# Layer 2's convolution units: x buffers in unit order, loads ahead of norms, raw strips for the last batch

## Chip, core and metric

The kernel runs on one core of one Trainium2 chip, in float32. The metric is the device time of one execution in microseconds (us). A core has five engines with queues of their own: TensorE (PE, with its weight loads as PEld), VectorE (DVE), ScalarE (ACT), GpSimd (POOL) and SyncE (SP). SP issues most DMAs here, ACT and POOL some. DMAs move data between device memory (HBM) and on-chip memory; PE writes its products to PSUM, from where ACT and DVE fetch them.

## What is computed

The input x has 4 batches, 384 channels and 64 x 64 positions. Four layers follow one another, each as x = x + f(gn(x)), where gn is a group norm without weights (32 groups, per batch). The change lies in layer 2 and at its borders:

```python
p = x.mean(axis=(2, 3), keepdims=True)            # here x is gn(x)
gate = sigmoid(sigmoid(bn(pw(gelu(bn(pw(p, dc_w1))), dc_w2))) - 0.5)
kw = softmax(bn(pw(gelu(bn(pw(p, kp_w1))), kp_w2)), axis=1)
y3 = bn(dw(x, c3_w, 1))                           # depthwise 3 x 3
y5 = bn(dw(x, c5_w, 2))                           # depthwise 5 x 5
y1 = x * c1_w + c1_b
tok = bn(kw[:, 0:1] * y3 + kw[:, 1:2] * y5 + y1)
tok = tok * sigmoid(bn(pw(gelu(bn(pw(tok.mean(...), cg_w1))), cg_w2)))
ch = tok + bn(pw(gelu(bn(pw(tok, cm_w1))), cm_w2))
return gate * ch + (1.0 - gate) * x
```

Every bn takes its mean and variance over all batches and positions, so a channel's two convolutions must be complete before its tokens can be formed, and all tokens before the matrix products that follow.

## The kernel before

The kernel is written with tile pools. A pool hands out buffers by tag (`bufs` of them), the waits between engines are generated, and the order in which instructions stand in each engine's queue is settled when the kernel is built; it need not be the order of the Python text. Channels lie on the 128 partitions, in three channel tiles j = 0, 1, 2.

**Phase A** (`phase_a`, layers 0 and 1) does attention and then layer 1, one batch at a time. The last batch's layer 1 (`layer1` with `alone`) runs by itself, in eight blocks of 512 positions. A block ends in `band_out` (L1142): for each channel tile o, two matrix products (L1148, L1149), an add on DVE into x[:, o] (L1152), then the statistics (L630) and a store of the block to x1 (L1155). When the eight blocks are done, `norm_of_stats` gives scale r2 and shift n2 of layer 2's group norm (L1026 to L1030). Beside it `strips_of` already prepares batches 0 to 2 of channel tile 0 for layer 2.

**Strips.** `open_strips` (L1161) holds z, 128 channels by 33 strips by 4 batches, with positions on the partitions and the batch innermost. A strip is a transposed 128 x 128 piece of normalised x. For channel tile 0, `strips5` (L1316) loads x1, normalises it on ACT (L1320), transposes it on PE (L1325) and copies it to z, in turn on ACT and DVE (L1331, L1329).

**Phase B** (`phase_b`, L1169) is the convolution stage. It works in 12 units of 32 channels; a unit's x tiles have 32 channels of each of four batches on the partitions. Unit u belongs to channel tile j = u // 4. Each unit has 16 steps of two channels:

- `matrices53` (L1339) forms, three steps ahead, the band matrices of a pair of channels from taps, on DVE or (odd steps) on POOL (L1351). `taps53` (L1333) loads the taps of four steps, one group ahead, by POOL (L1337), into one of three buffers.
- `conv53` (L1359) does 12 products with strips as stationary operand (L1370), two ACT copies out of PSUM (L1379, L1381), DVE statistics (L1384), and every fourth step a 1024 KB write to d53 from ACT's queue (L1386).
- `conv_norms` (L1391), after the next unit's first convolution, turns the statistics into coefficients.
- `unit_tok` (L1427) forms the tokens of the unit before, in four parts of two halves: it reads 1024 KB of convolution results back (c_d, three buffers, SP, L1436), adds on ACT and DVE into the unit's x tile (L1444, L1449, L1451), squares it (L1456) and stores the tokens (L1463).
- `unit_strips` (L1261) brings in x of a unit ahead: tile 0, then tile 1, each by eight SP loads of 128 KB (L1272), each norm on ACT for 1024 positions (L1280), then, for j > 0, transposes and copies to z (L1294, L1299, L1301).

The x tiles come from pool b_x, six buffers with one tag. A unit's two tiles are held from load to token store. `phase_b` asks for them in this order: four times for the last batch's strips of channel tile 0 (L1190), then unit 1's tile 0, unit 0's tile 0, unit 1's tile 1, unit 0's tile 1, then units 2, 3 and so on. The load of unit u + 2's first tile and its first norm come together at step 15 of unit u (L1218), its second tile at step 1 of the next unit. The token halves of unit u - 1 are drawn at the even steps of unit u and at step 15.

**The tail.** After unit 11 come its `conv_norms`, its tokens, `tok_stats` (L1466) and, in `phase_ef`, a chain of small operations up to the first product of the next stage (h_s, L1604). `phase_ef` first loads the weights w2 (cm_w2_t, 1152 KB, used only in its second half, L1660) and then w1, all from ACT's queue (L334).

## Time and profile before

| | |
|---|---|
| Runs (3), median | 4841.11 us (4838.23 to 4847.09) |
| Profiled execution | 4841.52 us |
| Its span | 4839.6 us, granted PE clock 0.95 |
| PE, DVE, ACT, POOL busy over the span | 91%, 60%, 41%, 16% |
| Last block's x1 done; norm ready | 2434.2; 2439.9 us |
| First convolution product (L1370) | 2460.19 us |
| Last unit's statistics on PE (L1402) | 3013.47 us |
| First product of the next stage (L1604) | 3067.74 us |
| Moved between 2460 and 3012 us | 154.70 MB, 280 GB/s |

Times are counted from the start of the span. A row of the timeline reads: start, length, engine and line, operation, what is written and read, count, and in brackets how long the engine was idle before and what released it. SPq is the queue from which SP issues DMAs; an issue's length is not the transfer's. In rows of stretches, the number behind each length in brackets counts instructions, and the DMA share is the mean busy share of 16 DMA engines. In a chain of waits each row is a start, a length and what that time went to.

### The profile page before, as it was taken

What the parts mean: (1) busy time and instruction counts of PE and PEld (TensorE: products, weight loads), DVE (VectorE), ACT (ScalarE), POOL (GpSimd) and SP (SyncE); (2) the same over time, 40 slices, a digit from 0 to 9 for tenths busy, and PEclk for the clock granted to TensorE, in tenths of its full rate; (3) what the DMA queues carried; (4) which work ended last, traced back from release to release, by engine and by line L of the source; (5) the groups of instructions that cost most, each with busy time, mean ns of one, the idle gap of its engine ahead of it and who ended that gap; (6) DMA issues with size and microseconds to landing.
All of it is one profiled execution on the core that took longest, in us unless ns stands there. A gap on an engine that the chain in (4) does not pass through costs nothing.

```text
span 4839.6 us, 49747 instructions
## 1 busy us (share of the span) xinstructions
PE 4399.5 (91%) x18445; PEld 2453.7 (51%) x18445; DVE 2892.0 (60%) x4647; ACT 1996.9 (41%) x2976; POOL 757.7 (16%) x643
## 2 busy tenths in 40 slices
PE   6999999999999999989987898699999997778888
PEld 2233444344443444435477787344444443678888
DVE  7766556645656455556867777555521113767898
ACT  4444444444444444336345566211133334763321
POOL 1000000000000000000044554000000001235544
PEclk9999999999999999989988999899999998788999
DMA  4312212111211111113168898776664444995776
GB/s 145 102 42 66 72 53 75 64 56 42 70 61 63 40 59 59 53 63 120 65 197 282 278 308 299 273 259 251 238 236 153 156 156 152 325 346 183 231 256 232
DMA packets 289663, 747.65 MB, mean 154 GB/s; under 512 B 22555, under 2 KB 123014, under 8 KB 277382
## 3 DMA queue, kind: packets, MB, share of 16 engines
q1 hardware_dynamic: 226744, 454.62, 29.4%
q0 software_dynamic: 36480, 167.01, 9.2%
q10 hardware_dynamic: 26190, 122.76, 6.4%
q8 instruction: 149, 2.44, 0.2%
q14 instruction: 100, 0.82, 0.1%
HBM read 442.04 MB, written 302.25 MB: 154 GB/s over the span
## 4 chain that ended last, share of the span: by engine, by line
PE 32%; DVE 7%; DMA 6%; ACT 3%; issue 2%; POOL 1%; SPq 0%; ACTq 0%; DVEq 0%; POOLq 0%
PE h_m L1658 10%; PE h_s L1604 10%; PE conv_m L1370 6%; PE conv_m L1972 2%; DMA c_d<-d 2%; DMA wmix<-in_mix_t 1%; DMA g_h<-h 1%; DVE toep L1959 1%; PE box_m L2050 1%; DVE in_x L2052 1%; DMA ax<-x 1%; DVE in_x L2062 1%; DMA unit_x<-x 1%; DVE box L2034 0%; ACT g_h L1908 0%
## 5 line engine op out<-in xcount | busy, mean ns | idle before, releaser
L819 ACT ACTIVATE probs<-sc_s 128x1024 f32<-128x1024 f32 x512 | 496.5, 1019 | 695.0 <-PE av L929 594.8
L929 PE MATMUL av<-probs,vt 128*128 128x512 f32 x1536 | 717.7, 604 | 0.0
L1128 DVE SCALAR_TENSOR_TENSOR acc<-band,vecs,acc 128x512 f32<-128x512 f32 x708 | 496.0, 745 | 44.9 <-POOL band L1089 39.6
L1658 PE MATMUL h_m<-f_h,cm_w_t 128*128 128x512 f32 x1152 | 497.3, 595 | 7.4 <-ACT f_h L1646 7.4
L1370 PE MATMUL conv_m<-toep,z 128*128 128x192 f32 (+1 forms) x2304 | 444.2, 354 | 9.5 <-DVE z L1299 9.4
L929 PEld LDWEIGHTS av<-probs,vt 128*128 128x128 f32 x1536 | 277.6, 192 | 339.6 <-issue 335.9
L1972 PE MATMUL conv_m<-toep,z 128*128 128x128 f32 x3072 | 395.5, 287 | 36.5 <-POOL toep L1959 15.8
L1370 PEld LDWEIGHTS conv_m<-toep,z 128*128 128x128 f32 x2304 | 408.5, 197 | 31.6 <-DVE z L1299 10.1
L1972 PEld LDWEIGHTS conv_m<-toep,z 128*128 128x128 f32 x3072 | 381.1, 203 | 38.4 <-POOL toep L1959 16.2
L1604 PE MATMUL h_s<-e_tok,cm_w_t 128*128 128x512 f32 x768 | 362.9, 595 | 4.2 <-DVE e_tok L1589 4.2
L1658 PEld LDWEIGHTS h_m<-f_h,cm_w_t 128*128 128x128 f32 x1152 | 220.4, 191 | 284.4 <-issue 273.3
L1666 DVE BATCH_NORM_STATS2 h_st<-f_h 128x6 f32<-128x512 f32 x96 | 66.5, 694 | 429.8 <-ACT f_h L1665 429.8
L811 PE MATMUL sc_s<-q,k 32*128 32x512 f32 x2048 | 307.1, 643 | 15.1 <-ACT probs L819 14.9
L1351 POOL TENSOR_TENSOR toep<-w,band 128x1280 f32<-128x1280 f32 x94 | 272.6, 2900 | 237.5 <-PE conv_m L1370 234.3
L1051 PE MATMUL t_m<-w_in_t,xb 128*128 128x384 f32 x768 | 282.0, 503 | 3.4 <-DVE coef L1068 3.2
L965 PE MATMUL proj_m<-xm,w_proj_t 128*128 128x512 f32 x576 | 270.3, 609 | 6.4 <-DVE xm L904 4.9
L1611 ACT COPY e_h<-h_s 128x1024 f32<-128x1024 f32 x96 | 97.2, 1012 | 400.2 <-PE h_s L1604 400.2
L1613 DVE BATCH_NORM_STATS2 h_st<-e_h 128x6 f32<-128x512 f32 x192 | 123.4, 685 | 204.9 <-ACT e_h L1611 204.7
L1604 PEld LDWEIGHTS h_s<-e_tok,cm_w_t 128*128 128x128 f32 x768 | 146.9, 191 | 187.9 <-issue 183.1
L1051 PEld LDWEIGHTS t_m<-w_in_t,xb 128*128 128x128 f32 x768 | 144.4, 194 | 141.6 <-issue 62.5
L972 DVE SCALAR_TENSOR_TENSOR x_res<-proj_m,bn_c,x_res 128x512 f32<-128x512 f32 x96 | 71.7, 747 | 240.2 <-PE proj_m L965 240.2
L1604 PE MATMUL h_s<-z,cm_w_t 128*128 128x512 f32 x384 | 196.7, 594 | 0.0
(423 smaller groups left out, 6396.3 us busy)
## 6 DMA issues: line engine op xcount, KB each, us to landing
d<-d_o ACTq DMA_DIRECT2D x48, 1024.0 KB
c_d<-d SPq DMA_DIRECT2D x48, 1024.0 KB
hid<-e_h ACTq DMA_DIRECT2D x16, 3072.0 KB
f_h<-hid SPq DMA_DIRECT2D x16, 3072.0 KB
x_in<-in_x SPq DMA_DIRECT2D x96, 256.0 KB
x_res<-in_x SPq DMA_DIRECT2D x32, 768.0 KB
xa<-x_res POOLq DMA_DIRECT2D x32, 768.0 KB, 3.9
xa_out<-xa SPq DMA_DIRECT2D x32, 768.0 KB
```

The source lines that it names most:

```text
L811: nc.tensor.matmul(s[:, g], lhsT=k4[32 * g : 32 * g + 32, c], rhs=q[i][32 * g : 32 * g + 32], start=True, stop=True,)
L819: nc.scalar.activation(p[:, h * 1024 : (h + 1) * 1024], s[:, 2 * h : 2 * h + 2].rearrange("p a b -> p (a b)"), AF.Exp, scale=0.25,)
L929: nc.tensor.matmul(av[0], lhsT=vt[:, 4 * c + v, :], rhs=p[:, v * 512 : (v + 1) * 512], start=c == 0 and v == 0, stop=c == 7 and v == 3,)
L965: nc.tensor.matmul(m, lhsT=self.w_proj[:, j, o * P : (o + 1) * P], rhs=xm[:, j], start=j == 0, stop=j == NJ - 1,)
L1051: nc.tensor.matmul(m[:, 0:C], lhsT=xb[:, j], rhs=self.w_in[:, j, :], start=j == 0, stop=j == NJ - 1,)
L1128: nc.vector.scalar_tensor_tensor(out, src(j, k), w, done, ALU.mult, ALU.add)
L1351: eng.tensor_tensor(t, self.w53[:, at : at + 160].rearrange("p (m n) -> p m n", n=8).unsqueeze(2).to_broadcast([P, 20, 8, 8]), band.rearra ...
L1370: nc.tensor.matmul(m[:, c * 256 + to : c * 256 + to + 64 * (k1 - k0)], lhsT=self.z_[:, at : at + P], rhs=t[:, 10 * c + k0 : 10 * c + k1].r ...
L1604: nc.tensor.matmul(s[:, v, :], lhsT=w1[:, j, o * P : (o + 1) * P], rhs=t[j][:, v * 512 : (v + 1) * 512], start=j == 0, stop=j == NJ - 1,)
L1613: nc.vector.bn_stats(st[:, o, 8 * b + 2 * i + v, :], h[:, o, v * 512 : (v + 1) * 512])
L1658: nc.tensor.matmul(m, lhsT=w2[:, o, j * P : (j + 1) * P], rhs=h[:, o, v * 512 : (v + 1) * 512], start=o == 0, stop=o == 5,)
L1972: nc.tensor.matmul(m[:, ch * P : (ch + 1) * P], lhsT=self.z_[:, at : at + P], rhs=t[:, 8 * c + 2 * i : 8 * c + 2 * i + 2].rearrange("p m a ...
```

## The change

- **Raw strips.** In the last batch's `band_out`, after the add of channel tile 0, `raw_strips` transposes the not yet normalised block (four transposes into a PSUM tile "m") and copies it to z by ACT.
- **Factors and scaling.** `strip_factors` builds, in phase B, the scale and shift of each of the 128 channels copied to every partition: two DVE operations, one product of 256 columns, one copy. It uses one x buffer. `scale_strips` multiplies and adds 32 channels of z in place on DVE, one quarter ahead of unit 0 and three at its steps 3, 7 and 11. The four loads, norms and strips of the last batch go.
- **Taps.** Their pool moves to `open_strips`, with two buffers for three, and the first load is issued there.
- **Order of x.** Unit 0's two tiles are asked for first (tile 0, norm, tile 1, ahead of the loop), unit 1's at steps 1 and 3. `load(0)` and `norm(0)` are apart by a yield: the load of unit u + 2 is drawn at step 11 and its norm at step 15.
- **Last unit.** Unit 10's token halves are drawn at every step from step 1 of unit 11, twice at even ones. Unit 11's four read-backs are asked for together, into x buffers, ahead of its `conv_norms`.
- **w2.** Its load moves from the start of `phase_ef` to POOL's queue after the second block of the next stage.

```diff
             nc.vector.tensor_add(x[:, o], x[:, o], m)
+            if o == 0 and b == B - 1:
+                self.raw_strips(b, h, x[:, 0])
             yield 2.0
...
+    def raw_strips(self, b, h, x):
+        m = self.pm("strip_m")
+        for k in range(4):
+            self.nc.tensor.transpose(m[:, k * P : (k + 1) * P], x[:, k * P : (k + 1) * P], self.ident)
+        self.nc.scalar.copy(self.z[:, :, 1 + 4 * h : 5 + 4 * h, b], m.rearrange("p (k c) -> p c k", c=P))
+
+    def strip_factors(self, b):
+        nc = self.nc
+        x = self.bx_p.tile([P, 2048], F32, tag="x", name="z_rep")
+        t, self.z_rep = (x[:, 256 * i : 256 * i + 256].rearrange("p (i c) -> p i c", i=2) for i in range(2))
+        for i, v in enumerate((self.r2, self.n2)):
+            nc.vector.tensor_scalar(t[:, i], self.ident, v[:, 0, b : b + 1], float(P), ALU.mult, ALU.mult)
+        m = self.pm("z_rep")[:, 0 : 2 * P]
+        nc.tensor.matmul(m, lhsT=self.mean128, rhs=t.rearrange("p i c -> p (i c)"), start=True, stop=True)
+        nc.vector.tensor_copy(self.z_rep, m.rearrange("p (i c) -> p i c", i=2))
+
+    def scale_strips(self, b, q):
+        at = slice(32 * q, 32 * q + 32)
+        zv = self.z[:, at, 1:33, b]
+        of = lambda i: self.z_rep[:, i, at].unsqueeze(2).to_broadcast([P, 32, 32])
+        self.nc.vector.tensor_mul(zv, zv, of(0))
+        self.nc.vector.tensor_add(zv, zv, of(1))
...
+        self.taps_s = ExitStack()
+        self.taps_p = self.taps_s.enter_context(self.tc.tile_pool(name="b_taps", bufs=2, side="right"))
+        self.taps53(0)
...
-            self.taps53(0)
             self.toep = {}
             for n in range(LEAD + 2):
+                if n == 2:
+                    self.strip_factors(B - 1)
+                    self.scale_strips(B - 1, 0)
                 self.matrices53(n)
-            for q in range(4):
-                x = self.bx_p.tile([P, 2048], F32, tag="x", name="in_x1")[:, 0:1024]
-                self.strips5(0, B - 1, x, 8 * q, self.pm)
...
-            strips, behind = self.unit_strips(1), None
-            next(strips)
+            first, strips, behind = self.unit_strips(0), self.unit_strips(1), None
+            for _ in range(3):
+                next(first)
...
-                tok = self.unit_tok(u - 1) if u else self.unit_strips(0)
+                tok = self.unit_tok(u - 1) if u else first
...
+                    if not u and n in (3, 7, 11):
+                        self.scale_strips(B - 1, n // 4 + 1)
...
-                    if n == 15 and u:
+                    if u == UNITS - 1 and n or u and n == 15:
                         next(tok, None)
+                    if not u and n in (1, 3):
+                        next(strips)
...
-                    if n == 15 and u + 2 < UNITS:
-                        strips = self.unit_strips(u + 2)
-                        next(strips)
+                    if n in (11, 15) and u + 2 < UNITS:
+                        if n == 11:
+                            coming = self.unit_strips(u + 2)
+                        next(coming)
+                        if n == 15:
+                            strips = coming
                 behind = st
+            results = [self.load_results(UNITS - 1, i, self.bx_p, "x") for i in range(4)]
             self.conv_norms(UNITS - 1, behind)
-            for _ in self.unit_tok(UNITS - 1):
+            for _ in self.unit_tok(UNITS - 1, results):
                 pass
...
         load(0)
+        yield
         norm(0)
         yield
...
-            self.w53_ahead = self.bt_p.tile([P, 8 * 80], F32, tag="w53", name="w53", bufs=3)
+            self.w53_ahead = self.taps_p.tile([P, 8 * 80], F32, tag="w53", name="w53", bufs=2)
...
-            w2 = self.weight(cp, "cm_w2_t")
+            w2 = cp.tile(list(self.ins["cm_w2_t"].shape), F32, tag="cm_w2_t", name="cm_w2_t")
...
+                    if b == 0 and i == 1:
+                        nc.gpsimd.dma_start(w2, self.ins["cm_w2_t"])
                     nc.gpsimd.dma_start(self.wx[b][:, :, blk], x)
```

More of the change, by code (lines that the diff above doesn't have):

```diff
@@ L1217, in phase_b @@
                         next(nets, None)
-                    if n == 15 and u + 2 < UNITS:
-                        strips = self.unit_strips(u + 2)
-                        next(strips)
+                    if n in (11, 15) and u + 2 < UNITS:
[4 more added lines that the diff above has]
+                            strips = coming
                 behind = st
+            results = [self.load_results(UNITS - 1, i, self.bx_p, "x") for i in range(4)]
             self.conv_norms(UNITS - 1, behind)
-            for _ in self.unit_tok(UNITS - 1):
+            for _ in self.unit_tok(UNITS - 1, results):
                 pass
             self.tok_stats()
+        self.taps_s.close()
     def units(self, pool):
@@ L1425, in conv_norms, with load_results, unit_tok @@
         self.tok_s = s, s0
-    def unit_tok(self, u):
+    def load_results(self, u, i, pool, tag):
+        d = pool.tile([P, 2 * 8 * P], F32, tag=tag, name="c_d").rearrange("p (y v n) -> p y v n", v=2, n=P)
+        self.nc.sync.dma_start(
+            d.rearrange("p y v n -> p y (v n)"),
+            self.d53[u][8 * i : 8 * i + 8].rearrange("y b c v n -> (b c) y (v n)"),
+        )
+        return d
+    def unit_tok(self, u, results=None):
         nc = self.nc
@@ L1433, in unit_tok @@
             sl = slice(i * 1024, (i + 1) * 1024)
-            d = self.bc_p.tile([P, 8, 2, P], F32, tag="d", name="c_d")
+            d = results[i] if results else self.load_results(u, i, self.bc_p, "d")
             o = self.unit_x[u][i // 2][:, i % 2 * 1024 : i % 2 * 1024 + 1024]
-            nc.sync.dma_start(
-                d.rearrange("p y v n -> p y (v n)"),
-                self.d53[u][8 * i : 8 * i + 8].rearrange("y b c v n -> (b c) y (v n)"),
-            )
             for h in range(2):
```

## The prediction, on record before the run

> **What bounds the kernel now.** I read the page first, then busy times stretch by stretch, then what ended each wait of TensorE (PE) and of SyncE's DMA queue (SPq), then the chain of waits at both ends of the stage.
>
> ```profile
> span 4839.6 us, 49747 instructions
> ```
>
> The change lies in layer 2's convolution stage, and the page's shares average over stages with other limits. So I cut the trace where each unit's norm statistics reach PE (L1402), which gives one row per unit.
>
> ```profile
> 2434.20:2460.20 26.00, 10.26 (x39) 7.37 (x39) 15.71 (x33) 9.50 (x10) 3.11 (x6) 0.50 0.85 255
> 2503.80:2539.90 36.10, 36.10 (x204) 34.49 (x205) 25.11 (x50) 17.51 (x41) 24.28 (x13) 1.00 0.80 263
> ...
> 2576.00:2639.30 63.30, 38.91 (x211) 35.77 (x210) 39.37 (x81) 36.51 (x73) 23.64 (x12) 0.78 0.95 313
> ...
> 2880.30:2925.80 45.50, 42.04 (x235) 39.27 (x235) 36.20 (x73) 29.02 (x62) 25.56 (x12) 0.95 0.90 300
> ...
> 3013.50:3067.70 54.20, 5.43 (x24) 4.51 (x24) 26.50 (x88) 24.25 (x44) 0.00 (x0) 0.51 0.87 287
> ```
>
> Columns: stretch, length, busy PE, PE loads, VectorE (DVE), ScalarE (ACT), GpSimd (POOL), clock, DMA share, GB/s. Unit 1 is pure PE, 36.1 us. Unit 3 takes 63.3 because PE waits for unit 4's strips. Unit 9 takes 45.5, with PE at 42.0 and DMA at 0.90. Ahead of the loop (26 us) and behind it (54 us) PE hardly works. All twelve units, 2460.2 to 3013.5, take 43.6, 36.1, 36.1, 63.3, 45.7, 49.8, 51.9, 45.9, 47.7, 45.5, 45.1, 42.6: 553.3 us.
>
> The SPq timeline and SPq's waits (total, times, longest, 2438 to 2530) say why unit 3 is late:
>
> ```profile
> 2440.95 84.43 SPq L1272 DMA_DIRECT2D unit_x<-x  x48
> 2525.42 2.68 SPq L1436 DMA_DIRECT2D c_d<-d  x3
> 2543.96 0.34 SPq L1463 DMA_DIRECT2D tok<-unit_x  x1
> ```
>
> ```profile
> SPq L1272 <- DMA d<-d_o: 51.8, 6, 20.3
> ```
>
> The loads of x for units 0 to 2 hold the queue until 2525.4, 51.8 us of it behind writes of convolution results. Unit 0's results, complete soon after 2504, are therefore read only from 2525.4, and its first token store leaves at 2544. A unit's x buffers come free only with its token stores, so later loads, norms and transposes inherit the lag. PE's timeline shows it in units 3 and 10:
>
> ```profile
> 2633.73 1.97 PE L1294 MATMUL strip_m<-ident,unit_x 128*128 128x128 f32 x8 [15.29 <-ACT unit_x L1280]
> ...
> 2968.68 1.10 PE L1294 MATMUL strip_m<-ident,unit_x 128*128 128x128 f32 x8 [2.31 <-ACT unit_x L1280]
> ```
>
> The chains of the opening and of the tail:
>
> ```profile
> 2439.92 6.68 DMA w<-in_c_t
> ...
> 2446.62 7.08 DVE toep L1351 x5
> ...
> 2460.19 1.86 PE conv_m L1370 x4
> ```
>
> ```profile
> 3012.15 7.80 DMA d<-d_o
> ...
> 3022.05 12.23 DMA c_d<-d
> ...
> 3038.36 9.99 DMA c_d<-d
> ...
> 3067.74 7.69 PE h_s L1604 x12
> ```
>
> The opening waits for taps, then five matrices, then strips. In the tail unit 11's fourth read-back (3038.4) waits for one of three buffers.
>
> **What the skill says.** The Trainium skill, "DMA: Bandwidth & Descriptors", Specifications: HBM gives a core about 358 GB/s. The trace's six 20 us stretches with a share of 0.97 or more moved 354, 329, 365, 335, 348 and 328: mean 343, the rate I use. "TensorE: Matmul & The Clock Gate", table at its head: ScalarE, VectorE and GpSimd queues are strict FIFO. So an ACT norm that waits holds what follows it; the trace has ACT at L1280 waiting 9.0 us for loads over the loop. "SBUF — State Buffer", Door 1: SBUF has 16-byte lines, and each access that crosses to a new one pays. Writing z at a 16-byte stride costs 1057 ns per 128x512 (L1331), with inner runs (L1301) 585 ns, which agrees.
>
> **The change, part by part** (savings negative).
>
> *Last layer-1 block, +1.5.* Eight times four transposes and one ACT copy come in. Warm transposes run eight in 1.04 us: 32 x 0.13 = 4.2 us PE; 8 x 1.06 = 8.5 us ACT. From 2200 to 2340 PE is busy 133 of 140 us, afterwards 82 of 94. Idle ACT (23 busy of 94) hides its part; about a quarter of PE's shows, plus possibly half of the last block's four cold transposes (1.1 us). These transposes wait for DVE's add; behind them on PE stand the out_m products of the next channel tiles, and the block's last add waits for those. Range 0 to +5. The early tap load and memsets on idle POOL cost nothing; without that cover, 0.6 us per issue.
>
> *Opening, -11.8.* Four loads, norms and strip groups go, and the 6.7 us tap wait. The norm is ready at 2439.9. Then on DVE: two matrices 3.0; two small scalings 0.5 (L1250: 0.25 each); a cold 256-column matmul 1.3 (144 columns: 0.85); copy 0.4; first quarter's multiply and add. No such in-place strided 1024-element pair is in the trace: at the matrices' 1.16 ns per element it is 2.4 us, at twice z's strided 2.07 ns it is 8.5. I take 3.2 for the pair, as the second input is broadcast. Convolution starts at 2448.4 instead of 2460.2. Bounds -14 to -6.
>
> *Unit 0, +2.4.* Three more quarters, 9.6 us of DVE (7 to 25), in a unit where DVE is busy 32.5 of 43.6. The free 11 us hide most; I take 46.0. At 25 us it costs 14.
>
> *Loop, units 1 to 11, -47.4.* Order and loads ahead are meant to end the lag: c_d of unit 0 need not queue behind unit 2's second tile, and a unit's first load gets four convolution steps before its norm. Moved from step 15 to 11, its eight issues (0.42 each, 3.4 us) stand on SPq ahead of two token parts' stores and reads; the cover is that the buffer's two stores left by step 8. Is it not free, those wait too, and the lag stays (third rival). The replicated factors hold one of six x buffers to step 11 of unit 0, before unit 2's second tile wants it: nothing. Floors per full unit: bytes are 4 x 1024 written, 4 x 1024 read back, 16 x 128 loaded, 4 x 512 stored, 4 x 320 taps = 13568 KB = 13.9 MB, at 343 GB/s 40.5 us; PE 36.1 + 32 x 0.13 = 40.3 us. Today's undisturbed units take 45.3, 5 us above. I expect half of that excess to stay, as DMA and PE are nearly equally full: 42.8. Units 1 and 2 lose their light load (0.80 share): 41 each. Units 3 to 10: 8 x 42.8. Unit 11, no strips: 38. With 46.0 the sum is 508.4, against 553.3: -44.9, unit 0 included. The second tap buffer's wait hides under three matrices ahead (about 7 us): landings took 3.1 to 10.0 us, a group lasts about 10. Uncovered, up to 3 us a group. Draining unit 10's tokens by unit 11's sixth step costs nothing while DVE has room there (32.6 of 42.6).
>
> *Tail, -13.* The chain's last write still lands 8 us after the loop. Four reads go at once: 4.2 MB at 343 GB/s is 12.2 us, plus 2 us latency, then one 3 us token step: done at about 3037.5 instead of 3051.2. The 16.5 us from there to the first h_s stay. A 1152 KB weight (3.4 us of DMA) leaves these same seconds for the next stage, where DMA is at 0.6 to 0.9 and PE at 20.0 of 20; POOL's issue of 0.7 us is hidden there, and if it were not, 0.7 is the cost. Bounds -4 (buffers still held by unit 10) to -16.
>
> **Sum:** 1.5 - 11.8 - 44.9 - 13 = -68.2. The profiled execution took 4841.5 us (span 4839.6, 1.9 around it), the median is 4841.1: they agree. 4841.5 - 68.2 = **4773.3**.
>
> **Rivals.** *All excess goes* (0.16): loop 46 + 2 x 40.5 + 8 x 40.5 + 36.1 = 487, -66; tail -15: 4750. For it: no single engine is above 40.5. Against: DVE needs 36 us per unit as well. *DMA is the wall already* (0.24): share 0.90 hides a queue that can't be packed tighter, units stay at 45.5; only unit 3 and 4 to 6's extra stalls go: 46 + 82 + 8 x 45.5 + 40 = 532, -21; tail -10: 4800. For it: 10 loads take 11 us to issue in late units. *The change doesn't reach the lag* (0.07): x loads again stand behind result writes; loop +2, opening -6, block +2, tail -5: 4834. *Slower* (0.10): the norm at step 15 stands in ACT's FIFO ahead of PSUM evacuations; where x lands later than four steps (about 10 us) after step 11, ACT stops, and PE after its four banks. Ten units at 5 us on top of today's loop: 553 + 50, less 23 at the ends: 4868. It decides above 2.3 us per unit; against it, only 9.0 us of such waits in all today.
>
> **How the numbers follow.** Forecast 0.43. About 0.2% (10 us) is what can be told from no change: faster 0.43 + 0.16 + 0.24 = 0.83, same 0.07, slower 0.10. The range takes the three fast cases with their bounds: 4742 to 4815, leaving 0.17 out.
>
> **What would show it.** Right: first convolution near 2449; unit 0's first token store before its successor is half done; unit 3 near 43 us; no 15 us strip wait; four c_d issues together, and 42 us from last convolution to h_s. Wrong: strip multiplies above 3 us each; SPq's x loads waiting for d; ACT L1280 waiting for loads; late units still at 45 us with DMA at 0.9.

## The result, and the profile after

| | before | after |
|---|---|---|
| Median (20 runs each) | 4838.57 us | 4841.42 us |
| Ratio after / before, 95% interval | | 1.0000 (0.9992 to 1.0009) |
| Span of the profiled execution | 4839.6 us | 4844.5 us |

There is no change that can be measured. The forecast was 4773.3 us, with a range of 4742 to 4815, so it was wrong by 68 us. The sum of its steps is compared with the two profiles below. Rows are stretches between marks that both traces have: first tap product of the last layer-1 batch, norm ready, first convolution, a unit's statistics on PE, first product of the next stage.

| Stretch | before | after | difference | predicted |
|---|---|---|---|---|
| first tap product of the last batch to norm ready | 234.8 | 243.5 | +8.7 | +1.5 |
| norm ready to first convolution | 20.3 | 12.6 | -7.7 | -11.8 |
| unit 0 | 43.6 | 49.3 | +5.7 | +2.4 |
| units 1 to 11 | 509.7 | 518.7 | +9.0 | -47.4 |
| last statistics to first h_s | 54.3 | 43.6 | -10.7 | -13 |

The differences sum to +5.0. The profiled execution of after began the last batch's taps 2.9 us earlier and lost 2.8 us behind h_s; with these the sum is the spans' difference of 4.9. Two stretches gained 18 us, three lost 23.

These rows of stretches of the changed kernel answer to those of before: opening, units 1, 3 and 9, tail.

```profile
2440.25:2458.29 18.04, 2.73 (x14) 2.02 (x14) 16.27 (x34) 0.50 (x2) 1.49 (x3) 0.61 0.82 213
2507.64:2547.97 40.33, 39.52 (x213) 37.23 (x213) 26.27 (x51) 17.45 (x41) 26.23 (x13) 0.96 0.80 256
2584.61:2654.28 69.67, 38.68 (x210) 35.47 (x210) 43.65 (x88) 38.82 (x76) 23.16 (x12) 0.77 0.83 275
2889.32:2935.31 45.99, 44.19 (x247) 41.63 (x247) 36.33 (x74) 27.94 (x61) 25.57 (x12) 0.94 0.88 284
3026.28:3069.84 43.56, 5.04 (x24) 4.12 (x24) 22.02 (x80) 20.45 (x37) 0.58 (x1) 0.52 0.93 313
```

The opening is shorter and now full of DVE work (16.3 of 18.0 us). Unit 3, which was to fall to 43 us, went from 63.3 to 69.7. Unit 9 stayed at 46. Only the tail came close to its figure. SPq's timeline and its waits from 2440 to 2553 us show that the lag of before is still there:

```profile
2445.21 86.99 SPq L1312 DMA_DIRECT2D unit_x<-x  x48
2532.30 2.56 SPq L1470 DMA_DIRECT2D c_d<-d  x3
2552.10 0.34 SPq L1508 DMA_DIRECT2D tok<-unit_x  x1
```

```profile
SPq L1312 <- DMA d<-d_o: 60.7, 5, 33.1
SPq L1508 <- DVE unit_x L1496: 17.2, 1, 17.2
```

It is the picture of before: 48 loads of x ahead of the first read-back, and waits for result writes, 60.7 us of them for 51.8. Behind the read-backs unit 0's first token store waits another 17.2 us for DVE (15.8 in before). One wait for a result write is 33.1 us long, up to 2493, and for 12 us of it DMA moves nothing at all: the row of what DMA moved from 2440 to 2560 us (slices of 3 us) shows the hole from 2464 to 2476.

```profile
GB/s 104 198 238 231 235 254 229 61 0 0 0 0 136 331 0 3 272 191 249 213 251 75 372 272 138 0 191 268 209 330 206 254 289 361 390 400 309 149 224 362
```

PE's timeline in unit 0, unit 3 and unit 10:

```profile
2475.70 4.60 PE L1411 MATMUL conv_m<-toep,z 128*128 128x256 f32 x12 [4.94 <-issue]
...
2646.91 1.97 PE L1335 MATMUL strip_m<-ident,unit_x 128*128 128x128 f32 x8 [22.13 <-ACT unit_x L1320]
...
2976.03 1.97 PE L1335 MATMUL strip_m<-ident,unit_x 128*128 128x128 f32 x8 [5.23 <-ACT unit_x L1320]
```

The strip waits are still there, 22.1 us for 15.3 in unit 3. In the tail's chain of waits, the read-backs that were to go together do not:

```profile
3024.70 5.67 DMA d<-d_o
...
3030.86 10.59 DMA tok<-unit_x
3041.59 8.38 DMA c_d<-d
...
3069.84 8.23 PE h_s L1649 x12
```

Units 10 and 11 hold four of six x buffers, so not all of unit 11's read-backs have one; the last leaves at 3041.6 us, behind 10.6 us for a token store of unit 10 to land.

### The profile page after: what moved, and what is told of

It is laid out like the page before. It is cut to its first block, busy times and chain, and to the rows that moved or that the text cites. A ratio compares the mean times of both kernels' runs of the same rounds, so it can differ in the third digit from the quotient of the medians.

```text
span 4844.5 us, 49738 instructions
## 1 busy us (share of the span) xinstructions
PE 4396.7 (91%) x18447; PEld 2451.9 (51%) x18447; DVE 2909.2 (60%) x4654; ACT 1994.1 (41%) x2976; POOL 757.3 (16%) x644
## 5 line engine op out<-in xcount | busy, mean ns | idle before, releaser
L1128 DVE SCALAR_TENSOR_TENSOR acc<-band,vecs,acc 128x512 f32<-128x512 f32 x708 | 494.0, 745 | 49.8 <-POOL band L1089 45.5
L2019 PE MATMUL conv_m<-toep,z 128*128 128x128 f32 x3072 | 393.7, 286 | 38.4 <-POOL toep L2006 16.9
L1392 POOL TENSOR_TENSOR toep<-w,band 128x1280 f32<-128x1280 f32 x94 | 276.1, 2938 | 240.3 <-PE conv_m L1411 234.8
```

Of the source, the lines that this page charges most:

```text
L1128: nc.vector.scalar_tensor_tensor(out, src(j, k), w, done, ALU.mult, ALU.add)
L1392: eng.tensor_tensor(t, self.w53[:, at : at + 160].rearrange("p (m n) -> p m n", n=8).unsqueeze(2).to_broadcast([P, 20, 8, 8]), band.rearra ...
L2019: nc.tensor.matmul(m[:, ch * P : (ch + 1) * P], lhsT=self.z_[:, at : at + P], rhs=t[:, 8 * c + 2 * i : 8 * c + 2 * i + 2].rearrange("p m a ...
```

## The experiments

Each kernel ran beside the kernel before on one chip, but not all on the same chip, so ratios are compared and not medians. In the table, ratios are to the kernel before with their 95% interval; the other columns are from the profile of one execution each, in us: norm ready to first convolution, unit 0, unit 3, the mean of units 4 to 10, the tail. Spans are not compared: the first attention product av, which no edit touches, began at 63.7 us in the profile of before and at 86.1 in that of e1_order. f4_raw_only has all of the convolution stage as in before, and shows how far such columns vary by themselves: unit 3 63.8 and 63.3 us, tail 50.4 and 54.3.

The expectations name their theories by letters: S, loads wait for completion semaphores of result writes; Q, the order of the queues and the buffers; W, DMA is the wall; B and B2, what the raw strips and their scalings cost; T, the built order of the tokens; L, how long buffers are held; F, SP's single queue.

| Kernel | median | ratio | opening | unit 0 | unit 3 | units 4-10 | tail |
|---|---|---|---|---|---|---|---|
| before | 4838.6 | 1 | 20.3 | 43.6 | 63.3 | 47.4 | 54.3 |
| after | 4841.4 | 1.0000 (0.9992 to 1.0009) | 12.6 | 49.3 | 69.7 | 47.2 | 43.6 |
| e1_order | 4827.8 | 0.9966 (0.9954 to 0.9979) | 20.1 | 41.4 | 67.9 | 47.0 | 43.3 |
| e2_ends | 4852.6 | 1.0027 (1.0016 to 1.0039) | 12.6 | 51.9 | 64.0 | 48.5 | 52.7 |
| h3_last | 4830.9 | 0.9975 (0.9966 to 0.9985) | 20.5 | 43.2 | 68.0 | 47.7 | 41.8 |
| f4_raw_only | 4848.8 | 1.0016 (1.0007 to 1.0025) | 19.7 | 43.4 | 63.8 | 47.8 | 50.4 |
| f5_held | 4848.7 | 1.0016 (1.0007 to 1.0025) | 12.7 | 55.0 | 67.7 | 46.9 | 43.2 |
| g4_taps | 4827.3 | 0.9970 (0.9959 to 0.9981) | 15.9 | 43.2 | 64.8 | 47.2 | 43.7 |
| e3_d_pool | 4838.4 | 0.9996 (0.9985 to 1.0006) | 12.7 | 50.5 | 64.7 | 47.2 | 45.6 |
| e4_x_256k | 4845.1 | 1.0010 (0.9998 to 1.0021) | 12.6 | 55.4 | 66.3 | 47.5 | 48.5 |
| f0_prio | 4838.9 | 0.9998 (0.9987 to 1.0009) | 19.9 | 43.5 | 78.1 | 46.6 | 44.8 |
| f1_prio | 4837.8 | 0.9996 (0.9981 to 1.0010) | 19.9 | 41.4 | 77.9 | 46.1 | 44.6 |
| g3_more | 4908.8 | 1.0144 (1.0125 to 1.0163) | 20.0 | 60.8 | 79.3 | 46.8 | 43.8 |
| h1_dump | 4830.9 | 0.9973 (0.9960 to 0.9985) | 19.5 | 42.2 | 65.0 | 47.4 | 43.7 |
| g2_half | 4776.5 | 0.9864 (0.9848 to 0.9879) | 20.1 | 41.4 | 57.2 | 41.3 | 40.8 |
| g1_x7 | 4823.2 | 0.9965 (0.9954 to 0.9975) | 20.3 | 43.4 | 49.5 | 47.2 | 54.8 |
| g1c_d2 | 4870.8 | 1.0057 (1.0041 to 1.0073) | 20.3 | 43.1 | 65.4 | 51.4 | 56.4 |
| h5_act_tok | 4830.5 | 0.9980 (0.9971 to 0.9990) | 19.6 | 41.3 | 59.7 | 47.8 | 44.3 |
| h6_prio_act_tok | 4827.0 | 0.9974 (0.9961 to 0.9987) | 19.9 | 41.3 | 49.7 | 47.8 | 45.5 |
| h2_x7_last | 4819.4 | 0.9949 (0.9935 to 0.9962) | 20.7 | 43.5 | 51.0 | 47.4 | 50.5 |

### The parts, one by one

**e1_order**: the kernel before with the order of x alone.

```diff
-            strips, behind = self.unit_strips(1), None
-            next(strips)
+            first, strips, behind = self.unit_strips(0), self.unit_strips(1), None
+            for _ in range(3):
+                next(first)
...
-                    if n == 15 and u + 2 < UNITS:
-                        strips = self.unit_strips(u + 2)
-                        next(strips)
+                    if n in (11, 15) and u + 2 < UNITS:
+                        if n == 11:
+                            coming = self.unit_strips(u + 2)
+                        next(coming)
+                        if n == 15:
+                            strips = coming
```

> The kernel before with one part of the change: x buffers in unit order and loads four steps ahead of norms. Theory S (slots: SP's x loads wait because each transfer of SP and ACT takes one of eight completion semaphores in turn, so that a load stands behind a convolution-result write that ACT has not issued yet): the loop gets slower or stays, unit 3 at 63 us or more, +5 to +20 us, about 4852 us. Theory Q (queue order and buffers alone set the lag): faster, -20 to -45 us. Theory W (DMA is the wall, the lag costs little): -5 to +5 us.

It is 0.34% faster, 16 us. None of the three theories has it so: the loop is 552.6 us, as before (553.3), and what the profile shows of a gain is the tail, 11.0 us, which no part of this edit names.

```profile
3027.91:3071.17 43.26, 5.04 (x25) 4.13 (x25) 22.04 (x80) 20.46 (x37) 0.00 (x0) 0.52 0.91 305
```

With the new order unit 10's tokens end earlier: its last token store leaves 3.4 us after the last statistics, for 17.9 in the kernel before. Buffers come free, and unit 11's fourth read-back leaves 13.5 us after the last statistics instead of 24.9. All twenty kernels agree with this: where unit 10's last token store leaves within 6 us of the last statistics, the tail is 40.8 to 45.6 us; where it leaves 16.8 us or more behind, 50.4 to 56.4 (in e4_x_256k, 10.7 and 48.5).

**e2_ends**: the changed kernel with just these lines turned back.

> The changed kernel with the order of x undone: raw strips, taps, last unit and w2 stay. If the ends gain what the two traces suggest (opening about -2 after the loss in the last layer-1 blocks, tail -11) and the loop is as before: 4826 us (4818 to 4836). Theory S: first three units as before, SP's x loads wait about 50 us for result writes. If the opening's scaling costs unit 0 more than it saves: 4835 to 4845.

It is 0.27% slower, outside the expected range. The opening gained its 7.7 us, but unit 0 took 51.9 us, the stretch ahead of the norm 245.4 us, and the tail 52.7: the last unit's part without the order does not shorten it, and unit 10's last token store leaves 21.8 us behind the last statistics. So the ends cost what the order gives: -0.34% and +0.27% make the zero of the change.

**h3_last**: e1_order plus the last unit's part.

```diff
-                    if n == 15 and u:
+                    if u == UNITS - 1 and n or u and n == 15:
                         next(tok, None)
...
+            results = [self.load_results(UNITS - 1, i, self.bx_p, "x") for i in range(4)]
             self.conv_norms(UNITS - 1, behind)
-            for _ in self.unit_tok(UNITS - 1):
+            for _ in self.unit_tok(UNITS - 1, results):
```

> The kernel with the order of x alone plus the last unit's part (unit 10's token halves at every step, four read-backs at once), without raw strips, taps and w2. Account by parts: the tail was 43.3 us with the order alone and 43.6 us with all parts, so the last unit's part brings nothing on top: 4825 to 4830 us. If it does bring what the prediction gave it: -5 us or more, 4822 us or less.

0.9975 beside 0.9966: the last unit's part brings nothing that can be measured on top of the order. From here to the changed kernel (1.0000) only the raw strips with their scaling, the taps and w2 are added: they cost 0.25%, 12 us. w2 was not run alone.

**f4_raw_only**: the kernel before plus `raw_strips` in the last batch; strips as before overwrite what it writes.

```diff
+            if o == 0 and b == B - 1:
+                self.raw_strips(b, h, x[:, 0])
             yield 2.0
```

> The kernel before, with the raw transposes and their copies to z added in the last batch's eight blocks and nothing else; their content is overwritten afterwards by the strips as before, so the result is the same. From the start of the last batch's taps to the norm being ready the profiles show 234.8 us without and 243.6 to 245.9 us with raw strips. Theory B (the transposes cost PE their full 5.5 us and change the built order ahead of the last blocks): +9 to +11 us, 4849 to 4852 us. The prediction's figure: +1.5 us (0 to +5), 4842 us.

0.16% slower, about 8 us. First tap product to norm ready, of this kernel:

```profile
2208.01:2450.82 242.81, 216.46 (x714) 106.06 (x712) 181.36 (x276) 111.25 (x181) 10.51 (x24) 0.95 0.26 84
```

and of the kernel before:

```profile
2205.01:2439.85 234.84, 212.00 (x682) 104.10 (x680) 181.69 (x277) 103.61 (x173) 13.49 (x23) 0.94 0.27 87
```

PE is busy 4.5 us more, with 32 transposes that take 5.5 us, and all of it shows. The other 3.5 us are idle PE: its waits for DVE's sums between tap products grew from 4.5 us (6 waits) to 8.5 (9), and 2.9 us of waits for ACT's copies to z are new, while two other waits fell by 3.9 us together. That the transposes move the last blocks' products and leave less other work to fill DVE's chains is my reading; it was not tested.

**f5_held**: the changed kernel with scalings kept behind the statistics of their step.

```diff
-                        self.scale_strips(B - 1, n // 4 + 1)
+                        with self.tc.issue_after(self.stat.ins):
+                            self.scale_strips(B - 1, n // 4 + 1)
```

> The changed kernel with the three later scalings of strips held behind the statistics of their step on DVE, so that they cannot move ahead of matrices. Theory B2 (the six operations of 2.0 us that were brought forward in one piece starve PE of matrices in unit 0): unit 0 from 49.3 to 43 to 45 us, total -4 to -6 us, about 4836 us. If unit 0 is long because DVE is full however they stand: within 2 us of 4841 us.

Theory B2 fell here, and the other expectation too: at 1.0016 it is some 8 us slower than the changed kernel. The profile of after has all six later scalings between 2458.8 and 2477.3 us, with PE's stall of 4.9 us in it, and I took that bunching for the cause. Spread out, unit 0 takes 55.0 us, and PE waits 6.4 us for statistics and 4.9 us ahead of a small product instead. In both, DVE has some 12 us more to do than in e1_order: 45.6 of 55.0 us, and 44.7 of 49.3 in the changed kernel, for 33.2 of 41.4. That this load is the cause is my reading.

**g4_taps**: e1_order plus the early tap load with its two buffers.

```diff
         self.nc.gpsimd.memset(self.z_[:, P * 132 : P * 132 + 4], 0.0)
+        self.taps_p = self.taps_s.enter_context(self.tc.tile_pool(name="b_taps", bufs=2, side="right"))
+        self.taps53(0)
```

> The kernel with the order of x alone, plus the early tap load alone (pool and first load move to the opening of the strips; strips of the last batch as before). Theory: the tap wait of 5.9 to 6.7 us goes and nothing stands in its place on PE or DVE; if strips then end last, 2 to 4 us of it come: 4822 to 4826 us. If the early load costs in the last layer-1 blocks as the raw strips do: 4828 us or more.

The opening falls by 4.2 us to 15.9, and units 0 to 2 give 4.7 us back (43.2, 37.1, 38.1 for 41.4, 36.2, 36.1): 0.9970, no difference to e1_order. Of the 4.7, unit 0's 1.8 may be no effect: h3_last, without the tap edit, has 43.2 there too.

### What holds the loop

**e3_d_pool**: the changed kernel with result writes from POOL's queue.

```diff
-            nc.scalar.dma_start(
+            nc.gpsimd.dma_start(
                 self.d53[u][:, :, 2 * n - 6 : 2 * n + 2]...
```

> The changed kernel with the convolution-result writes issued by POOL instead of ACT, nothing else. Theory S: SP's x loads no longer wait for result writes, the 48 loads are out by about 2470 us, unit 0's results are read from about 2510 us, unit 3 falls below 50 us, the loop to 510 to 535 us, total 4785 to 4815 us; POOL's waits for ACT may take some of it back. Theory Q: the read-back still starts near 2530 us and unit 3 stays above 60 us, 4835 to 4850 us. Theory W: unit 3 falls, but the late units stay at 45 to 46 us with a DMA share of 0.9, about 4810 to 4820 us.

In the built program, and in the traces, every transfer of SP and ACT takes one of eight completion semaphores in turn and first waits for the transfer that had it; that is how an x load, which needs no result, came to wait for a result write. With POOL issuing the writes, it no longer does:

```profile
2454.22 39.08 SPq L1312 DMA_DIRECT2D unit_x<-x  x48
2521.31 2.71 SPq L1470 DMA_DIRECT2D c_d<-d  x3
2559.07 0.34 SPq L1508 DMA_DIRECT2D tok<-unit_x  x1
```

```profile
SPq L1508 <- DVE unit_x L1496: 35.0, 1, 35.0
```

The loads are out by 2493.3, and the read-backs leave as unit 0 ends. Yet unit 3 takes 64.7 us and nothing is won: the first token store still comes 38 us after the read-backs, behind a 35.0 us wait for DVE. So theory S names a real wait that was not the one that counts. The built order of DVE's queue says why: unit 0's eight token additions stand 15.5 to 28 steps behind the unit's end, in before, after and e1_order alike (15 to 32 for unit 1). What SP's queue gives, DVE's takes.

**e4_x_256k**: the changed kernel with four x loads of 256 KB per tile.

```diff
-            for k in range(2):
-                at = i * 2048 + k * 1024
-                for b in range(B):
...
+            for b in range(B):
+                nc.sync.dma_start(x[32 * b : 32 * b + 32], self.x1[b][32 * q : 32 * q + 32, j, i * 2048 : i * 2048 + 2048])
```

> The changed kernel with a unit's x tile loaded by four transfers of 256 KB instead of eight of 128 KB. Theory S: half as many completion semaphores are taken in turn, fewer loads stand behind result writes and each still can; the first three units gain 0 to 15 us, total 4820 to 4842 us. Theory Q: the order on the queue is the same, within 5 us of the changed kernel. Theory W: the same bytes, within 5 us.

1.0010: no gain, as theories Q and W had it.

**f0_prio** and **f1_prio**: the kernel before, and e1_order, with read-back, token halves and store under high priority. Unit 0's first addition then stands 4.5 steps behind the unit's end.

```diff
+            with self.tc.high_priority():
                 d = self.bc_p.tile([P, 8, 2, P], F32, tag="d", name="c_d")
                 ...
```

> The kernel before, with only the token halves, their read-backs and stores given high priority when the order of the queues is settled (unit 0's first token addition on DVE then stands 4.5 steps behind its unit's end instead of 15.5, and the first read-back behind 32 x loads instead of 48). Theory T (the lag is written into the built order of DVE's and SP's queues, whatever the order of x buffers): unit 3 falls from 63 to 40 to 48 us, the late units keep 43 to 46, the tail is 43 us as in the kernel with the order of x alone; total 4795 to 4815 us. Theory W (DMA is the wall in this stage and evens it out): unit 3 falls, but the next units give it back, 4825 to 4840 us. Theory S (slots of completion semaphores): reads and loads still stand behind result writes, unit 3 above 55 us.

> The kernel with the order of x alone, plus the same priority for the token halves. Theory T: both parts aim at the same lag, so it is within 8 us of the kernel before with the priority alone, 4790 to 4810 us. If order and priority add: 4780 to 4795 us. Theory W: about 4828 us, as with the order alone.

Theory T fell: in f1_prio the first token store leaves at 2513.9 us, 58.0 us after the first convolution, for 93.8 in the changed kernel, and unit 3 grows to 77.9 (78.1 in f0_prio). Its SPq in unit 3, and the wait on PE:

```profile
2601.53 0.34 SPq L1473 DMA_DIRECT2D tok<-unit_x  x1
2602.81 0.38 SPq L1444 DMA_DIRECT2D c_d<-d  x1
2603.24 1.43 SPq L1278 DMA_DIRECT2D unit_x<-x  x1
2607.91 0.33 SPq L1473 DMA_DIRECT2D tok<-unit_x  x1
2608.29 0.47 SPq L1278 DMA_DIRECT2D unit_x<-x  x1
```

```profile
2636.71 1.97 PE L1301 MATMUL strip_m<-ident,unit_x 128*128 128x128 f32 x8 [33.91 <-ACT unit_x L1286]
```

Unit 4's x loads now leave one by one between token stores that wait for DVE; the lag has moved from the tokens to the loads on the same queue.

**g3_more**: e1_order with every tap load made twice.

```diff
+            spare = self.bt_p.tile([P, 8 * 80], F32, tag="spare", name="spare", bufs=1)
+            self.nc.gpsimd.dma_start(spare, src.rearrange("p c m n -> p (c m n)"))
```

> The kernel with the order of x alone (4827.8 us), where every load of taps is made a second time into a buffer that nobody reads, by POOL: 1280 KB more per unit, 9% more bytes, at 343 GB/s 3.8 us of transfer; taps have two buffers for three. The order of all other instructions stays. Theory W (bytes bound the units: DMA is full or nearly so over a unit): +3 to +4 us in each unit from 3 on, +25 to +40 us in all, 4855 to 4868 us. Theory L (latency: the life of an x buffer through load, norm, transposes, tokens and store bounds the units, and the transfers have room): +0 to +10 us, 4828 to 4838 us.

It is 1.8% slower than e1_order (1.0144 and 0.9966), some 85 us, but not for its bytes: all spare loads were issued in units 0 to 3 (24 or so instructions on POOL per unit for 13), where they kept POOL from its matrices: PE waited 59.2 us for these. Units 4 to 10 are as without. The run says nothing on bytes.

**h1_dump**: e1_order with a second write of a quarter of the results.

```diff
+            nc.scalar.dma_start(self.dump[u][:, n // 4], self.d_o[:, 0:2].rearrange("p c v n -> p (c v n)"))
```

> The kernel with the order of x alone (4827.8 us), where a quarter of each block of convolution results is written a second time, by ACT, to an array that nobody reads: 1024 KB more per unit, 7.5%, tied to its unit because it can't start before the results are there. Theory W (bytes bound units 3 to 10): at 300 to 343 GB/s +3.1 to +3.5 us in each of these eight, +25 to +35 us, 4853 to 4863 us. Theory L (the life of an x buffer, not the bytes): 0 to +10 us, below 4838 us.

Moved bytes in the loop go from 157.35 to 169.07 MB, and the ratio from 0.9966 to 0.9973, inside both intervals; units 4 to 10 take 47.4 for 47.0. Theory W fell: the bytes of a unit alone do not bound the late units, though DMA's share in them is 0.9.

**g2_half**: e1_order without every second read-back.

```diff
-            d = self.bc_p.tile([P, 8, 2, P], F32, tag="d", name="c_d")
+            if i % 2 == 0:
+                d = self.bc_p.tile([P, 8, 2, P], F32, tag="d", name="c_d")
```

> The kernel with the order of x alone, leaving out every second read-back of convolution results, so that a unit's tokens use half of them twice and the result is wrong: 2048 KB fewer per unit, 15% fewer bytes, 6.1 us of transfer at 343 GB/s. Theory W: units 3 to 10 get shorter by 5 to 6 us until PE's 40.3 us stops them: unit 3 to 55 us or less, late units 41 to 42, total 4770 to 4790 us. Theory L: the order in the queues stays late, units 44 to 46, total 4810 to 4825 us.

The only edit that took the mean of units 4 to 10 below 46 us, to 41.3: 41.0 us each from unit 6 on, at a DMA share of 0.85, PE 39.7 us of it at full clock.

```profile
2763.08:2804.11 41.03, 39.69 (x235) 37.49 (x235) 35.89 (x74) 28.63 (x63) 25.54 (x13) 1.00 0.85 289
```

So 42.8 us can be reached, but with half the read-backs. The total lies where theory W had it, yet h1_dump speaks against bytes alone. Bytes are only one thing that this edit takes away; it also frees read-back buffers and waits, and the built order puts tokens at 4.5 to 16 steps. That order alone is not enough: h5_act_tok, below, has 4.5 to 17 and 47.8 us.

**g1_x7** and **g1c_d2**: e1_order with two read-back buffers for three, with and without a seventh x buffer.

```diff
-            self.bx_p = ctx.enter_context(tc.tile_pool(name="b_x", bufs=6))
+            self.bx_p = ctx.enter_context(tc.tile_pool(name="b_x", bufs=7))
-            self.bc_p = ctx.enter_context(tc.tile_pool(name="b_c", bufs=3))
+            self.bc_p = ctx.enter_context(tc.tile_pool(name="b_c", bufs=2))
```

> The kernel with the order of x alone, with seven x buffers for six and, to make room, two buffers for read-backs in place of three. Theory L: a tile's life may be a sixth longer, unit 3 below 60 us, late units 43 to 44, 4800 to 4815 us, unless the lost read-back buffer costs as much. Theory W: buffers don't matter, 4825 to 4840 us.

> The kernel with the order of x alone and two buffers for read-backs in place of three, six x buffers as before. With seven x buffers as well the loop took 535.8 us and the tail 54.8. If the seventh x buffer brought the loop's 17 us and the missing read-back buffer the tail's 11: loop 553 us or more, tail about 55 us, 4838 to 4845 us. If the read-back buffers changed the loop too: loop nearer to 540 us.

With two read-back buffers, the seventh x buffer is worth 0.92% (1.0057 to 0.9965), 45 us: unit 3 falls from 65.4 to 49.5 us, and units 4 to 10 from 51.4 to 47.2. With six x buffers, the third read-back buffer is worth 0.91% (1.0057 to 0.9966), again through units 4 to 10 (51.4 to 47.0). So how long buffers of both pools are held counts, as theory L has it. But its range for g1_x7 was missed (0.9965, and late units of 47.2 for 43 to 44), and what a seventh x buffer or a fourth read-back buffer would bring with the other pool at its present size was not run. My expectation for g1c_d2 named the tail as the place of its cost; it was the late units as well, and the total came 26 us above the range.

**h5_act_tok** and **h6_prio_act_tok**: e1_order and f1_prio with token stores issued by ACT.

```diff
-            nc.sync.dma_start(self.tok[u, :, :, sl]...
+            nc.scalar.dma_start(self.tok[u, :, :, sl]...
```

> The kernel with the order of x alone (4827.8 us), with the token stores issued by ACT, behind the square that needs the same data, instead of SP. Theory F (SP's single queue holds x loads behind token stores that wait for DVE): SP's waits for DVE go, in units 4 to 10 the built order has a unit's first tokens 4.5 steps behind its end and the last at 17, x comes in time, late units 41 to 43 us, total 4790 to 4808 us; unit 3 stays above 55 us, since unit 0's tokens still stand 15.5 steps behind. Theory S (completion slots): x loads still wait for result writes, late units 45 or more, 4822 to 4832 us.

> The kernel with the order of x and high priority for the tokens (4837.8 us), with the token stores issued by ACT. Theory F: with the stores off SP's queue, early tokens free x buffers early, in the first units too: unit 3 at 45 to 50 us, late units 41 to 43, loop 490 to 510 us, total 4775 to 4795 us. If read-backs, which stay on SP's queue ahead of x loads and wait for buffers and results, hold x as the stores did: unit 3 above 55 us, total 4800 to 4830 us.

With the stores alone (h5_act_tok) the late units stay at 47.8 us. With both edits unit 3 falls from 77.9 to 49.7 us, as theory F had it. But units 1 and 2 rise to 38.4 and 47.0 us (36.2 and 36.1 in e1_order), with DMA at a share of 0.97 and 1.00, so that units 0 to 3 together gain only 5 us: 176.4 for 181.6. The seventh x buffer did more, 164.8 in g1_x7. The late units do not follow either: 47.8. PE's waits in h5_act_tok from 2700 to 2940 us, and in h6_prio_act_tok over units 3 to 10:

```profile
PE cn_rep L1409 <- DVE st L1391: 27.1, 5, 5.4
```

```profile
PE conv_m L1377 <- DVE z L1306: 34.5, 8, 4.9
PE cn_m L1418 <- DVE cn_four L1414: 7.4, 7, 1.1
```

No strip waits for x any more, where in e1_order 23.2 us of PE's waits over units 4 to 10 were of that kind. Instead PE waits once a unit for DVE: in h5_act_tok about 5.4 us for statistics, in h6_prio_act_tok about 4.3 us for the last copy to z, which stands in DVE's queue behind tokens and statistics. One wait took the place of another, and h6_prio_act_tok is no faster than e1_order (0.9974 and 0.9966).

**h2_x7_last**: e1_order, seven x buffers, two read-back buffers, the last unit's part.

> The order of x, seven x buffers, two read-back buffers, and the last unit's part, whose four read-backs go to x buffers and so don't need the missing one. If the loop's 536 us and a tail of 43 to 46 us add up: 4812 to 4816 us. If the tail stays at 54 us: 4822 us.

0.9949, the fastest version with all of the computation: 25 us below the kernel before. The tail is 50.5, not 43 to 46.

## Why the prediction was wrong

**Loop, -47.4, measured +9.0.** This step failed, and it carries 56 of the 73 us between the sum (-68.2) and the two profiles (+5.0). The sentence that failed is "Order and loads ahead are meant to end the lag: c_d of unit 0 need not queue behind unit 2's second tile". It does queue there. The code says so without any run: unit 2's second tile is asked for in step 1 of unit 1, unit 0's first read-back in step 2. The change moved first tiles only. Nor is that queue all of the lag. The trace of before had a second wait of SPq from 2438 to 2545 us, which the prediction did not use:

```profile
SPq L1272 <- DMA d<-d_o: 51.8, 6, 20.3
SPq L1463 <- DVE unit_x L1451: 15.8, 1, 15.8
```

Unit 0's first token store waits for DVE, where its token additions stand 15.5 to 28 steps behind the unit's end, before and after the change. e3_d_pool, whose 48 loads were out 26 us after the first convolution, for 74 in after, got only a longer wait for DVE (35.0 us for 17.2). There a term that the step had put at nothing shows as well: an x load waits 11.1 us for the last scaling, since the factors still hold an x buffer. Unit 3, forecast at 42.8 us, thus makes 26.9 of the 56 us.

SPq's block of 48 loads ahead of three read-backs is what the third rival described, and its 4834 us lay within 8 us of the result, in part by luck: its block was too cheap (2 us for 8.7) and its tail too small (-5 for -10.7). I gave it 0.07, since I took what the order was meant to do for what it did.

Units 4 to 10 make 30.6 more, and here the second half of the step failed. "I expect half of that excess to stay, as DMA and PE are nearly equally full": all of it stays, also in h6_prio_act_tok, where tokens come early, and in g1_x7, where a seventh x buffer bears the lag. In all kernels but g2_half and g1c_d2, units 4 to 10 take 46.1 to 48.5 us, against floors of 40.5 and 40.3. (Unit 11 adds 3.7, and units 1 and 2 give 5.1 back.) The second rival had this ("units stay at 45.5"), but for a wrong reason: what 7.5% more bytes cost could not be measured. Part of the excess is the clock. The Trainium skill, "TensorE: Matmul & The Clock Gate", Part 1, says that the clock falls to half after an idle window of some 3.4 us; the trace agrees: in unit 10 of after, eight transposes behind a wait of 5.2 us took 1.97 us, for 1.04 warm. With the same 234 PE instructions per unit, PE was busy 42.2 us on the mean of units 4 to 10 of after at a granted clock of 0.92, for 40.0 in g2_half at 0.99: 2 us of the excess.

**Block, +1.5, measured +8.7 and, alone, 0.16%.** "About a quarter of PE's shows" failed: in f4_raw_only PE's work showed whole, and another 3 to 4 us of waits came with it. The range given, 0 to +5, was too narrow. The windows had PE busy for 133 of 140 us; cover was assumed on PE itself, where there was none.

**Opening, -11.8, measured -7.7.** The loads, norms and the tap wait went as forecast; a term of the sum was too small. The pair of scalings took 3.9 us for the 3.2 taken. But the sum had two matrices ahead of it, and the built order put all five on DVE first or in between, as this timeline of DVE in after shows:

```profile
2446.57 2.88 DVE L1392 TENSOR_TENSOR toep<-w,band_p 128x1280 f32<-128x1280 f32 x2
...
2453.01 1.96 DVE L1183 TENSOR_TENSOR z<-z,z_rep 128x1024 f32<-128x1024 f32 x1
2454.89 1.48 DVE L1392 TENSOR_TENSOR toep<-w,band_p 128x1280 f32<-128x1280 f32 x1
2456.28 1.96 DVE L1184 TENSOR_TENSOR z<-z,z_rep 128x1024 f32<-128x1024 f32 x1
```

Three more matrices of 1.48 us are 4.4 us, the miss; the smaller differences nearly cancel. The scaling's 1.9 ns per element, for 1.16 in the matrices, agrees with the Trainium skill, "SBUF — State Buffer", Door 1, which has a penalty on accesses that cross to a new line (z's other strided copy: 2.07 ns). The prediction took less because the second input is broadcast; 1.9 ns shows little of that.

**Unit 0, +2.4, measured +5.7.** "The free 11 us hide most" failed. Three quarters took 11.9 us of DVE for the 9.6 taken, and PE waited for DVE's work in both places that were tried for the scalings (after and f5_held). DVE was busy 44.7 of 49.3 us in after. How much of the loss is this load, and how much the meeting of DVE and POOL (last section), no run separates.

**Tail, -13, measured -10.7.** The number was nearly right by luck, the reason wrong. e1_order has the same tail without the last unit's part, e2_ends with that part and without the order has 52.7, and h3_last adds nothing that can be measured. "Four reads go at once" did not happen with six x buffers. That unit 10's tokens drain earlier, which the sum gave no worth, goes with a short tail in all twenty kernels.

**What stays open** is what sets the late units. Bytes of a unit, waits for completion semaphores behind result writes, the place of tokens and the queue of their stores are each excluded as the single cause; when the wait for x was taken away, another of 4 to 5 us per unit appeared. That several in-order queues close in turn is my reading of it, and it is not shown further than h5_act_tok and h6_prio_act_tok show it for DVE. The buffers are not excluded: one less in either pool cost 4 us per late unit, and no run had more of one pool without less of the other. Which property of the read-backs makes 41 us possible in g2_half was not tried, and neither was the token edit of h6_prio_act_tok without the order of x.

## What to carry to other kernels

When a change is said to let one thing go ahead of another, list the steps at which each is asked for, and look whether the pair changes places, in the queue of every engine on its way: here DVE's order held what SP's gave. A stage at 0.9 of DMA and 0.9 of PE need not be bound by bytes: add some before calling it full. When one unit gets shorter, sum its neighbours too; the wait may have moved there. And work that is added to an engine that is busy nearly all the time should be priced whole: 5.5 us on a PE that was busy 133 of 140 us came to 8 us here.

## What the runs showed of the hardware

- In after DMA moved nothing for some 12 us on end (2464 to 2476 us), while 22 x loads of the first 48 had not left and SP waited for a result write. Such a hole is not by itself a loss: in e3_d_pool the 48 loads were out 39 us earlier, at the same time in all (0.9996 and 1.0000).
- DVE and POOL block each other where they meet: in f5_held a scaling of 1024 elements took 4.58 us, for 1.96 elsewhere, while POOL formed two matrices in 9.14 us, for 2.87 each elsewhere; in the changed kernel an operation of DVE on 12 x 1 elements took 2.79 us while POOL formed one. The Trainium skill has the mechanism, and the prediction did not use it: "SBUF — State Buffer", SBUF: two separate sides, says that DVE instructions with two inputs in SBUF and GpSimd instructions that read SBUF share a pair of ports, which one of them holds for a whole instruction. The scalings and the small operation have two such inputs; the durations agree.
- An unchanged stretch, start to first attention product, differed by 22 us between two profiled executions; stretches from a common mark in unchanged code agreed within 4 us (before and f4_raw_only).
